# Tap weights computed in quarters of the TensorE array and kept in SBUF, with the products spread one by one

## The chip, the cores and the metric

The kernel runs on one core of one Trainium2 chip. The core's engines are TensorE (PE, with its weight loads shown apart as PEld), VectorE (DVE), ScalarE (ACT), GpSimd (POOL) and SyncE (SP), which here only issues transfers. Each engine works through its own instructions in order and meets the others at semaphores. The metric is the device time of one execution in microseconds, as the median of several runs; less is better. The profile is one execution of its own, and its times are those of that execution.

## The reference, cut to what matters

The input `x` has 8 images of 256 channels and 64 x 64 pixels, fp32. Two layers follow one another, each as `x = x + layer(group_norm(x))`.

Layer 0 makes, for every pixel and every one of 32 channel groups, nine weights ("tap weights") out of a small network, and uses them on the 3 x 3 neighbourhood of a map `x3`:

```
h  = relu(bn2(conv1x1(relu(bn1(concat(x1, unfold3(x2)))), cw1)))   # 32 channels
w  = conv1x1(h, cw2) + cb2                                         # 32 groups x 9 taps
out[group, s] = sum over k of w[group, k] * unfold3(x3)[group, s, k]   # 8 channels s in a group
```

Layer 1 is local attention over 7 x 7 neighbourhoods (queries, keys, values, softmax), plus a branch with nine softmax weights per channel and pixel. In this branch all nine maps are nearly the same, so the kernel needs only one depthwise result times a quotient: with the weights taken relative to tap 4, the sum of eight exponentials plus one, limited to 1e37, and its reciprocal.

## The kernel before, in words

**Bands.** An image is cut into 8 bands (`NB`) of 8 rows, so there are 64 bands. The main loop runs over `g` from -12 to 63. In iteration `g` layer 1 works on band `g`, and layer 0 works ahead of it: the value maps of band `g + 12`, the hidden maps of band `g + 11`, and the tap weights and products of band `g + 10`. For `g` below 0 layer 0 is alone (the "front"). For `g` from 0 to 53 both layers run side by side, and for the last ten bands layer 1 is alone.

**Places.** An iteration has 8 steps `s` (`STEPS`), and each step calls `advance()` six times, so a band has 48 places. There is no automatic scheduling: the order in which the Python code issues instructions is the order in which each engine runs them. `after(n, f)` puts a piece of work `n` places later. `beside(g, s)` returns lists of what runs at the head, middle and end of a step, and `steer(g, s)` issues loads.

**Hidden map.** `hidden_maps` (from L413) ends in `relu` (L440), one ACT instruction that writes the hidden map of a band into `h2n[i % 2]`. This tile has 128 partitions, because the 8 rows of a band are split into 4 quarters of 2 rows, each with its 32 channels on 32 partitions. A row of the tile has two columns of padding, which makes 132 elements.

**Tap weights and products.** `tap_weights` (L463) takes a group of taps: two at a time beside layer 1, three at a time in the front (`TG`, L36). For each tap it issues one matmul (L470) of the block-diagonal 128 x 128 weights `c2[:, tap]` with the hidden map into a PSUM tile `pw`, which comes from the pool `gen` with four buffers, shared with nearly all other matmul results. PE runs a matmul in fp32 as two passes, and the profile counts both. Then `product` (L474) multiplies on DVE (L483): `prod = (pw[tap] + bias) * x3q[shifted]`, for 8 channels and 130 positions. Of its two tensor inputs `pw` lies in PSUM and `x3q` in SBUF. POOL adds the product to `xg` (L491), the sum over the taps. `prod` has two buffers. In the front every third product goes another way: PE adds it up in PSUM (L504). `TAPS_AT` (L67) says at the end of which steps the groups are issued, and `PRODUCTS_AT` (L68) how many places after that each product is. Beside layer 1 these are the ends of steps 1 to 5, and the products come one and two places after. When the last tap is in, `take` (L513) makes statistics and stores the band.

**Branch of layer 1.** `branch_weights` (L882) computes exponentials on ACT (L891) into `ex` (three buffers), POOL adds them up (L1106), and `dynamic_sum` (L893) makes the total (L899), its limit (L902), the reciprocal in two halves on DVE (L907), the two quotients on POOL (L908), and the product with the depthwise result `oc` (L912, L913). `depthwise_end` (L876) writes `oc` on ACT (L879). At the start of a band POOL also copies edges of the small map `x2` (L357 to L364), for which it waits for ACT (L347).

Of the kernel before, what the change touches and what calls it, by code (L numbers as in the profile page):

```python
# [10 lines left out]
F32 = mybir.dt.float32  # L11
# [7 lines left out]
P = 128  # L19
C = 256  # L20
# [16 lines left out]
SHARE = C // REL  # L37
PIECE = SR * W
RUN = (SR - 1) * (W + 2) + W
TG = 2, 3  # L40
HP = W + 2
HR = R + 2

# [20 lines left out]
STEPS = NCT * NT // 2  # L64


TAPS_AT = (1, 2, 3, 4, 5), (0, 2, 4)  # L67
PRODUCTS_AT = ((1, 2),) * 5, ((7, 14, 10), (9, 17, 13), (12, 20, 16))  # L68


CB3, CBQ, CBK, CBP, CWP0, CWP1, CW1, CW2, CBV = 0, 1, 2, 3, 4, 5, 6, 15, 24
# [16 lines left out]
def conv_layers_kernel(ctx: ExitStack, tc: tile.TileContext, ins: dict, out: bass.AP):  # L88
# [19 lines left out]
    def load(name, shape, src=None, now=True):  # L108
        t = const.tile(shape, F32, name=f"c_{name}")
        late.append(lambda: nc.scalar.dma_start(out=t, in_=ins[name] if src is None else src))  # L110
        if now:
            late.pop()()
        return t
# [8 lines left out]
    c1 = load("c1", [P, 3, REL])  # L122
    gq = load("gq", [P, P])
    gc = load("gc", [P, NCT, P])
    c2 = load("c2", [P, KK, P], now=False)
    wq = load("wq", [P, NCT, C], ins["wq"].rearrange("(t p) n -> p t n", p=P), now=False)
    wk = load("wk", [P, NCT, C], ins["wk"].rearrange("(t p) n -> p t n", p=P), now=False)
    wv = load("wv", [P, NCT, C], ins["wv"].rearrange("(t p) n -> p t n", p=P), now=False)
# [10 lines left out]
    x3n = [const.tile([P, R, HP], F32, name=f"x3n_{ct}") for ct in range(NCT)]  # L139

    h2n = [const.tile([P, SR, HP], F32, name=f"h2n_{i}") for i in range(2)]
    for t in probs + x3n + h2n:
        nc.gpsimd.memset(t, 0.0)

    def inverse_root(v):
# [45 lines left out]
    def layer1_loads():  # L191


        last = w1.tile([P, NCT, 1, C], F32, tag="oc", name="last")
        for f in late:
            f()
        nc.scalar.dma_start(out=last, in_=wfc_in[:, :, KK - 1 :])

        def first():
            nc.vector.tensor_scalar(wv, wv, rate1, None, ALU.mult)  # L200

        def difference(kt):
            nc.vector.tensor_sub(wfc[:, kt], wfc[:, kt], last[:, kt].to_broadcast([P, KK - 1, C]))

        return [first, lambda: difference(0), lambda: difference(1)]
# [12 lines left out]
    def after(n, f):  # L220
        later.append((place[0] + n, f))
# [191 lines left out]
    def hidden_maps(b, i, alone):  # L413

        im = images[b]
        hids = []
        h2 = h2n[i % 2][:, :, :W]

        def hidden(t):
            n = P if t == 0 else 96
            hid = w0.tile([P, R, W], F32, tag="hid", name=f"hid_{b}_{i}_{t}", bufs=2)
            nc.scalar.activation(
                hid[:n], im.x2[i][:n, t : t + R, :], AF.Relu, bias=bn1b[:n, t : t + 1], scale=bn1s[:n, t : t + 1]
            )
            hids.append(hid)

        def conv(home, first, last, start, stop):
            ph = home[:, 2 * P : 3 * P].rearrange("p (r c) -> p r c", r=SR)  # L430
            for t in range(first, last):
                n = P if t == 0 else 96
                for q in range(NQR):
                    nc.tensor.matmul(  # L434
                        ph[q * REL : (q + 1) * REL], c1[:n, t], hids[t][:n, q * SR : (q + 1) * SR],
                        start=(t == start), stop=(t == stop),
                    )
            return ph

        def relu(v):  # L440
            nc.scalar.activation(h2, v, AF.Relu, bias=bn2b, scale=bn2s)

        def one(home):
            ph = conv(home, 0, 2, 0, 1)
            after(1, lambda: hidden(2))
            after(2, lambda: nc.scalar.copy(h2, ph))

        def two(home):
            ph = conv(home, 2, 3, 2, 2)
            after(1, lambda: nc.vector.tensor_add(h2, ph, h2))  # L450
# [12 lines left out]
    def tap_weights(b, i, u, alone, at):  # L463


        im = images[b]
        first, n = TG[alone] * u, min(TG[alone], KK - TG[alone] * u)
        pw = ps.tile([P, n, SR * HP], F32, tag="gen", name=f"pw_{b}_{i}_{u}", bufs=4)
        for j in range(n):
            nc.tensor.matmul(  # L470
                pw[:, j], c2[:, first + j], h2n[i % 2].rearrange("p r c -> p (r c)"), start=True, stop=True
            )

        def product(j):  # L474
            k = first + j
            if alone and j == n - 1:
                prod = w1.tile([P, NCT, RP, W], F32, tag="yp", name=f"prod_{b}_{i}_{k}", bufs=3)
                prod = prod.rearrange("p t r c -> p (t r c)")[:, : SHARE * SR * HP]
                prod = prod.rearrange("p (s n) -> p s n", s=SHARE)
            else:  # L480
                prod = w0.tile([P, SHARE, SR * HP], F32, tag="prod", name=f"prod_{b}_{i}_{k}", bufs=2)
            at = k // 3 * HP + k % 3
            nc.vector.scalar_tensor_tensor(  # L483
                prod[:, :, :RUN], pw[:, j, :RUN].unsqueeze(1).to_broadcast([P, SHARE, RUN]),
                par[:, PCB2 + k : PCB2 + k + 1],
                im.x3q[i].rearrange("p s r c -> p s (r c)")[:, :, at : at + RUN], ALU.add, ALU.mult,
            )
            if alone and j == n - 1:
                after(9, lambda: gather(prod))
            else:  # L490
                nc.gpsimd.tensor_add(im.xg[i], im.xg[i], rows(prod))  # L491
            if k == KK - 2 + (not alone):
                if alone:
                    after(13, combine)
                after(14 if alone else 7, take)
# [379 lines left out]

    def depthwise_end(b, i, ct, acc):  # L876

        oc = w1.tile([P, BAND], F32, tag="oc", name=f"oc_{b}_{i}_{ct}")
        nc.scalar.activation(oc, acc.rearrange("p r c -> p (r c)"), AF.Copy, scale=rate2)  # L879
        return oc  # L880

# [11 lines left out]
    def dynamic_sum(b, i, ct, ex, oc):  # L893
# [5 lines left out]
        engine.tensor_add(tot, ex[:, 1], ex[:, 0])  # L899


        engine.tensor_scalar(tot, tot, 1.0, 1.0e37, ALU.add, ALU.min)  # L902
        rec = w1.tile([P, BAND // 2], F32, tag="rec", name=f"rec_{b}_{i}_{ct}", bufs=1)

        def quotient(u):
# [13 lines left out]
                out=out[b].rearrange("(t p) n -> p t n", p=P)[:, :, i * BAND : (i + 1) * BAND], in_=xr  # L919
            )  # L920

        after(9, lambda: quotient(0))
        after(13, lambda: quotient(1))
        after(15, weigh)


    def beside(g, s):
# [57 lines left out]
        if 0 <= g + AHEAD - 1 < B * NB and s == (2 if alone else 1):  # L985
# [5 lines left out]
                    convs.extend(parts)  # L991

            end.append(hidden)
        if 0 <= g + AHEAD - 2 < B * NB and s in TAPS_AT[g < -1]:
            u = TAPS_AT[g < -1].index(s)
            end.append(
                lambda: tap_weights(*divmod(g + AHEAD - 2, NB), u, g < -1, PRODUCTS_AT[g < -1][u])
            )
        return head, mid, end

    def steer(g, s):
# [128 lines left out]
def _layout(inputs):  # L1130
# [29 lines left out]
    arr["par"] = par  # L1160

    c2 = a["a_cw2"].reshape(REL, KK, REL).transpose(2, 1, 0)
    arr["c2"] = np.zeros((P, KK, P), f)
    for q in range(NQR):
        arr["c2"][q * REL : (q + 1) * REL, :, q * REL : (q + 1) * REL] = c2

    chan = np.zeros((C, NCHAN), f)
    chan[:, CB3] = a["a_b3"]
# [43 lines left out]
```

## Time and profile before

| | |
|---|---|
| median of 3 runs | 3852.04 us (3850.59 to 3853.89) |
| the profiled execution's own time | 3854.63 us |
| its span | 3852.8 us |
| instructions | 71646 |
| `pw` matmul passes (L470) | 1152 |
| products (L483), mean of one | 576, 1294 ns |
| additions of products on POOL (L491), mean of one | 549, 2185 ns |

The profile page gives each engine's busy time, the chain of work that ended last, and groups of instructions. In a group's line one reads: line, engine, operation, names of output and inputs, shapes, count, then the busy time in us and the mean of one in ns, and at the end the idle time of the engine just before these instructions and what ended it. Busy time overlaps between engines, so idle time matters only on the engine that sets the end. The timeline view lists instructions in order of time with their start and duration. The view by stretches gives, for a stretch of the execution, the busy time of PE, PEld, DVE, ACT and POOL with the number of instructions, then the granted clock, the share of time that the transfer engines were busy, and GB/s.

### The profile page before, as it was taken

The numbers are of one execution on the slowest core, as the hardware profiler recorded it, in microseconds if no ns is written. First come the engines' busy times: TensorE is split into PE (matmuls) and PEld (weight loads), VectorE is DVE, ScalarE is ACT, GpSimd is POOL, SyncE is SP. The second block draws the span as 40 slices with busy tenths as digits, with TensorE's granted clock in tenths as the row PEclk, the third lists the DMA queues.
The fourth block names the chain that finished last, engine by engine and source line by source line (L and its number), as shares of the span: only waits on it lengthen the run. The fifth ranks groups of instructions, "written<-read, shape, count | busy, mean of one in ns | idle before, by whom it ended". The sixth has DMA issues, their size and how long they took to land.

```text
span 3852.8 us, 71646 instructions
## 1 busy us (share of the span) xinstructions
PE 3756.3 (97%) x24620; PEld 2109.9 (55%) x24620; DVE 3434.4 (89%) x7125; ACT 2809.2 (73%) x6770; POOL 3116.8 (81%) x2100
## 2 busy tenths in 40 slices
PE   6889999999999999999999999999999999999998
PEld 3445555555555555555555555555555555555554
DVE  6879999999999999899998999999999899978877
ACT  4457777777777777777777777777777777677776
POOL 4868888888897888888888888888888888855565
PEclk9999999999999999999999999999999999999999
DMA  8764544544444544544544544454544544232221
GB/s 247 210 177 128 142 118 129 151 126 118 133 135 131 145 123 115 148 135 127 136 116 142 142 125 120 126 149 125 136 115 117 138 119 114 74 97 78 79 67 37
DMA packets 438926, 490.14 MB, mean 127 GB/s; under 512 B 62016, under 2 KB 324256, under 8 KB 438304
## 3 DMA queue, kind: packets, MB, share of 16 engines
q1 hardware_dynamic: 421984, 469.79, 44.1%
q10 hardware_dynamic: 16576, 15.76, 1.3%
q8 instruction: 194, 3.18, 0.4%
q14 instruction: 172, 1.41, 0.1%
HBM read 343.76 MB, written 145.10 MB: 127 GB/s over the span
## 4 chain that ended last, share of the span: by engine, by line
PE 81%; POOL 10%; DVE 3%; DMA 2%; ACT 2%; issue 2%; SPq 1%; ACTq 0%; POOLq 0%; DVEq 0%
PE pf L886 39%; PE small L799 6%; PE ptp L787 6%; POOL xg L491 6%; PE pk L706 5%; PE pq L684 5%; PE sco L750 5%; PE p L375 5%; PE pv L601 5%; PE pw L470 2%; POOL ex L1106 2%; PE small L332 1%; DVE prod L483 1%; PE small L434 1%; DMA x<-x3n 1%
## 5 line engine op out<-in xcount | busy, mean ns | idle before, releaser
L886 PE MATMUL pf<-yp,c_wfc 128*128 128x512 f32 x4096 | 1916.8, 594 | 11.3 <-DVE prod L483 6.3
L491 POOL TENSOR_TENSOR xg<-xg,prod 128x1024 f32<-128x1024 f32 x549 | 1199.8, 2185 | 132.5 <-DVE prod L483 103.6
L886 PEld LDWEIGHTS pf<-yp,c_wfc 128*128 128x128 f32 x4096 | 739.6, 190 | 711.4 <-issue 654.7
L1106 POOL TENSOR_TENSOR ex<-ex,ex 128x1024 f32<-128x1024 f32 x384 | 908.8, 2367 | 68.5 <-ACT ex L891 65.0
L891 ACT ACTIVATE ex<-pf 128x512 f32<-128x512 f32 x1024 | 604.0, 590 | 347.9 <-PE pf L886 269.2
L843 DVE SCALAR_TENSOR_TENSOR acc<-yp,c_chan,acc 128x504 f32<-128x504 f32 (+3 forms) x1104 | 775.5, 702 | 63.2 <-ACT acc L834 42.8
L483 DVE SCALAR_TENSOR_TENSOR prod<-pw,c_par,x3q 128x1040 f32<-128x1040 f32 x576 | 732.7, 1294 | 107.9 <-PE pw L470 60.8
L869 DVE SCALAR_TENSOR_TENSOR acc<-hid,c_chan,acc 128x504 f32<-128x504 f32 (+3 forms) x1024 | 751.1, 733 | 18.1
L781 ACT ACTIVATE prob<-prob,tot 128x196 f32<-128x196 f32 x1024 | 412.9, 452 | 242.4 <-DVE tot L779 236.8
L772 ACT ACTIVATE prob<-prob,nmax 128x196 f32<-128x196 f32 x1024 | 458.2, 450 | 101.3 <-DVE nmax L764 101.2
L907 DVE RECIPROCAL rec<-tot 128x256 f32<-128x256 f32 x256 | 445.7, 1741 | 28.3 <-POOL tot L902 27.5
L789 ACT COPY pt<-ptp 112x512 f32<-112x512 f32 x511 | 295.9, 579 | 111.8 <-PE ptp L787 111.8
L764 DVE CUSTOM_DVE_ANT_0 prob<-sco,c_mask 128x196 f32<-128x196 f32 x1024 | 324.8, 355 | 31.0 <-PE sco L750 31.0
L787 PEld LDWEIGHTS ptp<-ident,prob 128*112 128x112 f32 x2044 | 227.3, 133 | 184.4 <-issue 132.7
L787 PE MATMUL ptp<-ident,prob 128*112 128x128 f32 x2044 | 319.5, 279 | 0.0
L908 POOL TENSOR_TENSOR tot<-tot,rec 128x256 f32<-128x256 f32 x254 | 185.8, 732 | 145.7 <-DVE rec L907 139.7
L799 PEld LDWEIGHTS small<-pt,vt 112*64 112x64 f32 x8144 | 258.6, 138 | 79.8 <-issue 60.5
L799 PE MATMUL small<-pt,vt 112*64 112x64 f32 x8144 | 294.2, 225 | 3.3 <-DMA vt<-vd 1.8
L601 PE MATMUL pv<-c_wv,yp 128*128 128x256 f32 x1056 | 253.5, 383 | 1.8 <-ACT yp L572 1.8
L902 POOL TENSOR_SCALAR tot<-tot 128x512 f32<-128x512 f32 x127 | 243.9, 1920 | 11.1
L470 PEld LDWEIGHTS pw<-h2n,c_c 128*128 128x128 f32 x1152 | 175.1, 191 | 139.9 <-issue 115.9
L375 PE MATMUL p<-xc,w3s 128*128 128x512 f32 x512 | 243.3, 598 | 0.0
(136 smaller groups left out, 4656.7 us busy)
## 6 DMA issues: line engine op xcount, KB each, us to landing
vt<-vd SPq DMA_DIRECT2D x512, 112.0 KB
x3q<-x SPq DMA_DIRECT2D x128, 264.0 KB
xc<-in_x SPq DMA_DIRECT2D x64, 512.0 KB
xg<-in_xg SPq DMA_DIRECT2D x64, 512.0 KB
yp<-x SPq DMA_DIRECT2D x128, 256.0 KB
xr<-x SPq DMA_DIRECT2D x64, 512.0 KB
out_x<-xr SPq DMA_DIRECT2D x64, 512.0 KB
xs<-in_x SPq DMA_DIRECT2D x57, 512.0 KB
```

The lines of the kernel that those rows point to most:

```text
L483: nc.vector.scalar_tensor_tensor(prod[:, :, :RUN], pw[:, j, :RUN].unsqueeze(1).to_broadcast([P, SHARE, RUN]), par[:, PCB2 + k : PCB2 + k + 1],
L491: nc.gpsimd.tensor_add(im.xg[i], im.xg[i], rows(prod))
L601: nc.tensor.matmul(pv[:, g], yp[:, kt, r : r + 2].rearrange("p r c -> p (r c)"), wv[:, kt], start=(kt == 0), stop=(kt == NCT - 1),)
L772: nc.scalar.activation(prob[:, h, :NKEY], prob[:, h, :NKEY], AF.Exp, bias=nmax[:, h : h + 1], scale=-1.0, accum_out=tot[:, h : h + 1],)
L787: nc.tensor.transpose(ptp[:, h, ch], prob[:, h, ch * CHUNK : (ch + 1) * CHUNK], ident)
L799: nc.tensor.matmul(po[half[h], :, t * TQ : (t + 1) * TQ], im.vt[i + ch, m][:n, t, (2 * ct + h) * HD : (2 * ct + h + 1) * HD], pt[:n, h, ch ...
L843: nc.vector.scalar_tensor_tensor(o, yp[:, ct, ra + dr : rb + dr, ca + dc : cb + dc], chan[:, ct, CW1 + k : CW1 + k + 1], o, ALU.mult, ALU.add,
L869: nc.vector.scalar_tensor_tensor(o, hid[:, ra + dr : rb + dr, ca + dc : cb + dc], chan[:, ct, CW2 + k : CW2 + k + 1], o, ALU.mult, ALU.add,)
L886: nc.tensor.matmul(pf, wfc[:, kt, 2 * m + j, ct * P : (ct + 1) * P], images[b].yp[i][:, kt, PAD : PAD + R], start=(kt == 0), stop=(kt == N ...
L891: nc.scalar.activation(ex[:, j].rearrange("p (r c) -> p r c", r=R), pf, AF.Exp)
L907: nc.vector.reciprocal(rec, v)
L1106: after(4, lambda ex=ex, exb=exb: nc.gpsimd.tensor_add(ex, ex, exb))
```

## The change

The weights of a tap are block-diagonal in four blocks of 32. The change cuts the 128 x 128 matmul into four of 64 x 64, each with two of the blocks.

1. `c2` keeps only 64 columns: for each tap, rows 0 to 63 hold the blocks of quarters 0 and 1, rows 64 to 127 those of quarters 2 and 3. The blocks are the same for all quarters.
2. A second hidden map `h2s` holds the two halves of `h2` exchanged. `relu` writes it with two more ACT instructions on 64 partitions each, ahead of the one that writes `h2`.
3. Beside layer 1 there are now two groups of taps instead of five: taps 0 to 3 at the end of the last step of the iteration before, and taps 4 to 8 at the end of step 3 (`TAPS`, `TAPS_AT`). A group has two lots. The first lot uses rows 0 to 63 of the array and the second rows 64 to 127, each with its own PSUM tile; for each output half (64 columns of the array) the map comes from `h2` or `h2s`. So four matmuls of 64 x 64 for two taps stand next to each other. In the front a group still has three taps, all in the first lot.
4. Beside layer 1 `keep` copies the PSUM tiles to an SBUF tile `kept` on ACT, one copy a lot, one place after the matmuls. The products read `kept`, so both of their tensor inputs lie in SBUF. In the front they still read PSUM.
5. The products come one by one, 3, 8, 14 and 20 places after the first group and 2, 5, 8, 11 and 14 after the second.
6. In the last band of an image, for the first half of the channels, the limit on the sum of exponentials (L902) comes 5 places later; the first quotient follows 2 places later than before, the second quotient and the product with `oc` one place later.
7. `oc` (and the start-up tile `last` with the same tag) has one buffer instead of two.

```diff
-TG = 2, 3
+HALF = P // 2
...
-TAPS_AT = (1, 2, 3, 4, 5), (0, 2, 4)
-PRODUCTS_AT = ((1, 2),) * 5, ((7, 14, 10), (9, 17, 13), (12, 20, 16))
+TAPS = (((0, 1), (2, 3)), ((4, 5, 6), (7, 8))), tuple(((k, k + 1, k + 2), ()) for k in (0, 3, 6))
+TAPS_AT = (-1, 3), (0, 2, 4)
+PRODUCTS_AT = ((3, 8, 14, 20), (2, 5, 8, 11, 14)), ((7, 14, 10), (9, 17, 13), (12, 20, 16))
...
-    c2 = load("c2", [P, KK, P], now=False)
+    c2 = load("c2", [P, KK, HALF], now=False)
...
+    h2s = const.tile([P, SR, HP], F32, name="h2s")
-    for t in probs + x3n + h2n:
+    for t in probs + x3n + h2n + [h2s]:
...
         def relu(v):
+            for a, z in ((0, HALF), (HALF, 0)):
+                o, z = slice(a, a + HALF), slice(z, z + HALF)
+                nc.scalar.activation(h2s[o, :, :W], v[z], AF.Relu, bias=bn2b[z], scale=bn2s[z])
             nc.scalar.activation(h2, v, AF.Relu, bias=bn2b, scale=bn2s)
...
-        first, n = TG[alone] * u, min(TG[alone], KK - TG[alone] * u)
-        pw = ps.tile([P, n, SR * HP], F32, tag="gen", name=f"pw_{b}_{i}_{u}", bufs=4)
-        for j in range(n):
-            nc.tensor.matmul(
-                pw[:, j], c2[:, first + j], h2n[i % 2].rearrange("p r c -> p (r c)"), start=True, stop=True
-            )
+        lots = TAPS[alone][u]
+        ks = [k for lot in lots for k in lot]
+        n = len(ks)
+        pws = [
+            ps.tile([P, len(lot), SR * HP], F32, tag="gen", name=f"pw_{b}_{i}_{u}_{r}", bufs=4)
+            for r, lot in enumerate(lots) if lot
+        ]
+        side = [slice(0, HALF), slice(HALF, P)]
+        for m in range(len(lots[0])):
+            for q in range(2):
+                for r, lot in enumerate(lots):
+                    if m < len(lot):
+                        h2 = (h2n[i % 2] if q == r else h2s)[side[r]].rearrange("p r c -> p (r c)")
+                        nc.tensor.matmul(pws[r][side[q], m], c2[side[r], lot[m]], h2, start=True, stop=True)
+        weights = [pw[:, m] for pw, lot in zip(pws, lots) for m in range(len(lot))]
+
+        def keep():
+            kept = w0.tile([P, KK - 4, SR * HP], F32, tag="pw", name=f"kept_{b}_{i}_{u}", bufs=1)
+            for pw, lot, at in zip(pws, lots, (0, len(lots[0]))):
+                nc.scalar.copy(kept[:, at : at + len(lot)], pw)
+            weights[:] = [kept[:, j] for j in range(n)]
+
+        if not alone:
+            after(1, keep)
...
-                prod[:, :, :RUN], pw[:, j, :RUN].unsqueeze(1).to_broadcast([P, SHARE, RUN]),
+                prod[:, :, :RUN], weights[j][:, :RUN].unsqueeze(1).to_broadcast([P, SHARE, RUN]),
...
-        oc = w1.tile([P, BAND], F32, tag="oc", name=f"oc_{b}_{i}_{ct}")
+        oc = w1.tile([P, BAND], F32, tag="oc", name=f"oc_{b}_{i}_{ct}", bufs=1)
...
-        engine.tensor_scalar(tot, tot, 1.0, 1.0e37, ALU.add, ALU.min)
+        def limit():
+            engine.tensor_scalar(tot, tot, 1.0, 1.0e37, ALU.add, ALU.min)
+
+        late = 2 if (i, ct) == (NB - 1, 0) else 0
+        if late:
+            after(5, limit)
+        else:
+            limit()
...
-        after(9, lambda: quotient(0))
-        after(13, lambda: quotient(1))
-        after(15, weigh)
+        after(9 + late, lambda: quotient(0))
+        after(13 + late // 2, lambda: quotient(1))
+        after(15 + late // 2, weigh)
...
-        if 0 <= g + AHEAD - 2 < B * NB and s in TAPS_AT[g < -1]:
-            u = TAPS_AT[g < -1].index(s)
-            end.append(
-                lambda: tap_weights(*divmod(g + AHEAD - 2, NB), u, g < -1, PRODUCTS_AT[g < -1][u])
-            )
+        for gt, st in ((g, s), (g + 1, s - STEPS)):
+            front = gt < -1
+            if 0 <= gt + AHEAD - 2 < B * NB and st in TAPS_AT[front]:
+                u = TAPS_AT[front].index(st)
+                end.append(
+                    lambda gt=gt, u=u, front=front: tap_weights(
+                        *divmod(gt + AHEAD - 2, NB), u, front, PRODUCTS_AT[front][u]
+                    )
+                )
```

More of the change, by code (lines that the diff above doesn't have):

```diff
@@ L191, in layer1_loads @@
     def layer1_loads():
-        last = w1.tile([P, NCT, 1, C], F32, tag="oc", name="last")
+        last = w1.tile([P, NCT, 1, C], F32, tag="oc", name="last", bufs=1)
         for f in late:
@@ L466, in tap_weights @@
         im = images[b]
-        first, n = TG[alone] * u, min(TG[alone], KK - TG[alone] * u)
-        pw = ps.tile([P, n, SR * HP], F32, tag="gen", name=f"pw_{b}_{i}_{u}", bufs=4)
-        for j in range(n):
-            nc.tensor.matmul(
-                pw[:, j], c2[:, first + j], h2n[i % 2].rearrange("p r c -> p (r c)"), start=True, stop=True
-            )
+        lots = TAPS[alone][u]
[20 more added lines that the diff above has]
+            after(1, keep)
         def product(j):
-            k = first + j
+            k = ks[j]
             if alone and j == n - 1:
@@ L1162, in _layout @@
     c2 = a["a_cw2"].reshape(REL, KK, REL).transpose(2, 1, 0)
-    arr["c2"] = np.zeros((P, KK, P), f)
+    arr["c2"] = np.zeros((P, KK, HALF), f)
     for q in range(NQR):
-        arr["c2"][q * REL : (q + 1) * REL, :, q * REL : (q + 1) * REL] = c2
+        o = q * REL % HALF
+        arr["c2"][q * REL : (q + 1) * REL, :, o : o + REL] = c2
     chan = np.zeros((C, NCHAN), f)
```

## The prediction

> **What bounds the kernel now.** I began with the page's share of busy time and the chain that ended last.
>
> ```profile
> PE 3756.3 (97%) x24620; PEld 2109.9 (55%) x24620; DVE 3434.4 (89%) x7125; ACT 2809.2 (73%) x6770; POOL 3116.8 (81%) x2100
> PE 81%; POOL 10%; DVE 3%; DMA 2%; ACT 2%; issue 2%; SPq 1%; ACTq 0%; POOLq 0%; DVEq 0%
> ```
>
> TensorE (PE) sets the end, but DVE and POOL are not far behind. A mean over stages says little, so next came busy time in stretches: the front (47 to 233 us), and the middle of the run, where each band of layer 1 runs beside a band of layer 0 ten bands ahead.
>
> ```profile
> 47.00:233.00 186.00, 152.55 (x748) 79.77 (x748) 156.16 (x169) 86.13 (x160) 146.69 (x106) 0.93 0.75 207
> 1040.00:3220.00 2180.00, 2168.54 (x14443) 1227.93 (x14443) 1998.61 (x4173) 1655.22 (x4001) 1866.04 (x1246) 1.00 0.47 130
> ```
>
> The columns are PE, weight load, DVE, ACT, POOL. In 2180 us of the middle PE lacks 11 us of being always busy, DVE has 181 us to spare, ACT 525, POOL 314. I reckon in this stretch. Layer 1 with products beside it runs from 233 to 3349 us (54 bands of 57.7 us), so a gain or loss here counts 3116 / 2180 = 1.43 times.
>
> Third, the groups of the lines that the change touches, and POOL's waits in the stretch.
>
> ```profile
> L470 PE MATMUL pw<-h2n,c_c 128*128 128x132 f32 x1152 | 182.8, 280 | 1.8 <-ACT ex L891 1.8
> L750 PE MATMUL sco<-kb,qb 64*64 64x196 f32 x4096 | 235.4, 344 | 0.8 <-ACT qb L688 0.8
> L483 DVE SCALAR_TENSOR_TENSOR prod<-pw,c_par,x3q 128x1040 f32<-128x1040 f32 x576 | 732.7, 1294 | 107.9 <-PE pw L470 60.8 <-POOL xg L491 29.8 <-issue 16.1
> L491 POOL TENSOR_TENSOR xg<-xg,prod 128x1024 f32<-128x1024 f32 x549 | 1199.8, 2185 | 132.5 <-DVE prod L483 103.6 <-DVE sc_a L263 2.9 <-DMA yp<-x 2.8
> POOL x L357 <- ACT x L347: 170.1, 38, 6.4
> POOL xg L491 <- DVE prod L483: 57.0, 86, 1.7
> ```
>
> 1152 matmul records are 576 taps in two passes each, and a product per tap. POOL's 314 us of idleness are mostly one hole per band, before L357.
>
> Fourth, the operation that the trace of before nearly lacks: a DVE instruction with both tensor inputs in SBUF. A product today reads `pw` from PSUM. Only L205, in the front, reads two SBUF tensors. DVE's and POOL's instructions in order of time (start us, us):
>
> ```profile
> 55.60 4.20 DVE L205 TENSOR_TENSOR c_wfc<-c_wfc,last 128x2048 f32<-128x2048 f32 x1
> 71.55 2.28 DVE L205 TENSOR_TENSOR c_wfc<-c_wfc,last 128x2048 f32<-128x2048 f32 x1
> ```
>
> ```profile
> 50.97 6.68 POOL L491 TENSOR_TENSOR xg<-xg,prod 128x1024 f32<-128x1024 f32 x3
> 61.16 6.69 POOL L491 TENSOR_TENSOR xg<-xg,prod 128x1024 f32<-128x1024 f32 x3 [3.50 <-DVE prod L483]
> 68.66 2.17 POOL L491 TENSOR_TENSOR xg<-xg,prod 128x1024 f32<-128x1024 f32 x1
> 75.19 6.70 POOL L491 TENSOR_TENSOR xg<-xg,prod 128x1024 f32<-128x1024 f32 x3 [4.36 <-DVE prod L483]
> ```
>
> The same instruction takes 2.28 us while POOL stands idle (70.8 to 75.2), and 4.20 us when it starts 2.05 us before the end of a POOL addition (57.65). It ends 2.15 us after that addition: as if it had stood still until POOL was done. Products with one SBUF input show no such thing: 1.29 us, although most of them run under a POOL addition.
>
> [...] 64x64 scores start four at a time about 6.5 ns apart and a round of four takes 173 ns, while the slot of a 512-column pass grows from 429 to 522 ns when scores follow. [...]
>
> **The change part by part.**
> *Taps on PE.* Today a pass holds PE 113 ns (start to start), so a band costs 18 x 113 = 2034 ns. After, a band has rounds of up to four 64x64 matmuls: four for the first group, six for the second. A score round takes 173 ns for 196 columns, 10 more than the 163 that its columns take at the 429 ns of a 512-column pass; 132 columns take 111, so a round is about 120 and a band 10 x 120 = 1200 ns. Both groups stand directly ahead of scores, so the drain into this mode (93 ns) and the slow first round (224 instead of 173) are paid once, as now. Saved 0.83 us a band, 54 bands: 45 us while PE is the bound.
> *The front.* 27 groups keep three taps each, now 6 rounds of 120 instead of 6 passes of 113 ns, and switch mode alone (93 in, about 50 for the first round, 98 out): +0.28 us, 7.7 us in all. PE is 82% busy there, so 0 to 8; I take 4.
> *ACT.* Two 64-partition relus of about 0.48 us (today's L441 takes 482 ns) and four copies: from L446 (128 elements, 250 ns) and L789 (512, 579) three of 264 elements take 0.37 and one of 396 takes 0.48, so 2.5 us a band. ACT has 525 / 37.7 = 14 us a band to spare. The copies stand ahead of the exponentials of steps 0 and 4 and delay them by 0.7 to 0.85; without that cover the 2.5 us would be added.
> *Products in two SBUF inputs.* In the stretch 339 products start; by the records 87% of them start under a POOL instruction, with 0.79 us of it to run on average, and 1.14 of their 1.29 us overlap POOL. With a lock that overlap goes. DVE: L205 lost 1.92 of 2.05 us, so 0.79 - 0.13 = 0.66 us a product[...]: 1998.6 + 339 x 0.605 = 2204 us. POOL: a product reads for about 1.09 us (2.147 us for 2048 elements after POOL's end, times 1040 / 2048), and 87% hold POOL up: 1866.0 + 339 x 0.87 x 1.09 = 2187 us. Either exceeds the 2180 us that the stretch takes, before any idleness.
> *Places.* Products go one by one, from 3 places into step 0 (48 places a band, 1.2 us each), so the first two additions move into POOL's hole before L357. That absorbs the hole (170 + 32 us with L358), but not the other waits, 71 us for products and exponentials. In an in-order pair that now waits for each other I put remaining POOL idleness at half as much again, 105 us: 2187 + 105 = 2292, or +112 in the stretch, times 1.43 = +160 us. PE's 45 us are then worth nothing: it waits.
> *Late limit, one buffer for `oc` and for `kept`.* In eight bands L902 moves five places, the quotients two and one, the product with `oc` one. ACT's write of the next `oc` (L879) comes 0.7 us or more after POOL's read ends today; one place later or a slower POOL makes ACT wait, with the exponentials behind it. Between -8 and +8 us; I take 0 and leave POOL's lateness in the term above. `kept` is overwritten five places (6 us) after the first group's last product: a DVE more than that late would hold ACT too.
> *DMA queues.* No DMA moves but the store of the finished band, one place later; `x3q` is issued some 20 us ahead of the earlier first product. Half the bytes of `c2` are saved in the front. Nothing for these.
>
> Sum: 3852.8 + 160 + 4 = 4017 on the profiled execution, whose own time is 3854.6, 2.6 above the median of the runs; so I put the median at 4015 us.
>
> **The rivals.** *The lock doesn't hold for this instruction form* (0.20): L205 is one pair of records. Then PE stays the bound and gains 45 less 4: 3811 us, 3795 to 3838. This is the case on the other side; it decides if products keep 1.2 to 1.3 us under POOL's additions. *Contention that the new places mostly dodge* (0.10, of which 0.04 within 0.2%): the run is periodic, so products could regularly start as POOL ends or in its hole. Without extra idleness DVE's 2204 remains, +24 x 1.43: 3845 to 3890. [...] (0.08): POOL's instructions follow one another without a gap, mean 1.50 us (1866.0 / 1246). If half of the products are passed over once, DVE gets 170 x 1.5 = 255 more: 2459, +399 us, about 4250 and above. *ACT becomes the bound* through copies or `oc`: against it 14 us to spare a band; below 0.01 alone.
>
> **How the numbers follow.** Contention as reckoned has 0.62, its own range 3890 to 4250 us. A measurement of this kernel tells about 0.2% (8 us) from no change. Faster 0.20, same 0.04, slower 0.76 (0.62 + 0.08 + 0.06). For 8 in 10 the range takes in dodged contention (0.10), half of the passed-over case and a fifth of the fast one: 3825 to 4330.
>
> **What would show it.** Product records of 1.9 us mean instead of 1.29, with few at 1.24; POOL additions stretched by up to 1.1 us beyond 2.185 or starting late; PE below 97% busy in the middle, waiting on ACT and, behind it, on POOL and DVE; bands of 60 to 62 us; tap rounds of 120 ns. Were products to stay at 1.24 us beside unstretched additions, the prediction would be wrong, and bands near 56.9 us would follow.

## The result, and the profile after

The changed kernel takes 4177.29 us (median of 5 runs, 4169.86 to 4181.11). The kernel before took 3852.04 us in the same comparison. The ratio is 1.084, with an interval of 1.0825 to 1.0856: 325 us slower. The profiled execution's own time is 4179.14 us, its span 4177.3 us.

First the page of the changed kernel: busy time, then the chain that ended last, by engine and by line.

```profile
PE 3829.1 (92%) x25772; PEld 2058.8 (49%) x25772; DVE 3723.9 (89%) x7125; ACT 2920.1 (70%) x7118; POOL 3324.0 (80%) x2101
DVE 34%; PE 24%; POOL 16%; ACT 14%; issue 6%; DMA 5%; SPq 1%; ACTq 0%; POOLq 0%; DVEq 0%
DVE prod L506 13%; PE pf L909 12%; POOL xg L514 7%; DVE acc L892 6%; DVE rec L937 4%; DVE acc L866 4%; POOL ex L1140 3%; POOL tot L922 3%; PE small L822 2%; POOL tot L926 2%; PE sco L773 2%; DVE prob L787 2%; ACT x L349 2%; DMA vt<-vd 2%; ACT prob L804 2%
```

PE carried 81% of the chain before and carries 24% now. No engine has taken its place: DVE, PE, POOL and ACT share the chain, and the product (L506, L483 before) is its largest line. The same stretch of the middle as before, with the columns PE, weight load, DVE, ACT, POOL, then clock, DMA share and GB/s:

```profile
1040.00:3220.00 2180.00, 2011.56 (x13735) 1085.66 (x13734) 1997.58 (x3793) 1559.93 (x3828) 1824.37 (x1132) 0.98 0.44 118
```

PE now lacks 168 us of being always busy where it lacked 11. DVE is as busy as before (1998 us), but gets through 3793 instructions instead of 4173. POOL is less busy than before. In bands, counted from the first score of a band to that of the next, the mean of bands 1 to 52 grows from 57.67 to 63.56 us; in each of them DVE is busy 5.2 us longer (53.0 to 58.2) and POOL 3.7 us (49.7 to 53.4). Bands 0 to 53 take 3429.8 us instead of 3115.8, which is +314 of the +325 us. The front ends 6 us later, and the last ten bands take 4.5 us more.

The groups of instructions that answer to those shown of before, from the page and from the list with shapes kept apart:

```profile
L514 POOL TENSOR_TENSOR xg<-xg,prod 128x1024 f32<-128x1024 f32 x549 | 1217.5, 2218 | 457.4 <-DVE prod L506 428.3
L506 DVE SCALAR_TENSOR_TENSOR prod<-kept,c_par,x3q 128x1040 f32<-128x1040 f32 x495 | 947.8, 1915 | 94.0 <-POOL xg L514 57.9
```

```profile
L485 PE MATMUL pw<-h2n,c_c 64*64 64x132 f32 x1152 | 125.2, 308 | 5.7 <-ACT ex L914 3.2 <-DVE kb L744 2.5
L485 PE MATMUL pw<-h2s,c_c 64*64 64x132 f32 x1152 | 121.6, 308 | 0.6 <-DVE kb L744 0.3
L491 ACT COPY kept<-pw 128x264 f32<-128x264 f32 x165 | 56.9, 381 | 1.5 <-PE pw L485 1.5
```

A product that reads `kept` takes 1915 ns instead of 1294. POOL's own additions are hardly longer (2218 against 2185 ns), but POOL waits 428 us for products where it waited 104. POOL's longer instructions are elsewhere. These three groups, before and then after, are the total of the exponentials, its limit and the last sum of the branch:

```profile
L902 POOL TENSOR_SCALAR tot<-tot 128x512 f32<-128x512 f32 x127 | 243.9, 1920 | 11.1
L913 POOL TENSOR_TENSOR xr<-xr,oc 128x512 f32<-128x512 f32 x127 | 161.9, 1275 | 10.0
L899 POOL TENSOR_TENSOR tot<-ex 128x512 f32<-128x512 f32 x127 | 161.7, 1273 | 9.9
```

```profile
L926 POOL TENSOR_SCALAR tot<-tot 128x512 f32<-128x512 f32 x127 | 321.4, 2531 | 11.1
L922 POOL TENSOR_TENSOR tot<-ex 128x512 f32<-128x512 f32 x127 | 210.9, 1661 | 10.0
L943 POOL TENSOR_TENSOR xr<-xr,oc 128x512 f32<-128x512 f32 x127 | 196.6, 1548 | 10.0
```

None of the three was edited in its work, only the place of the limit in eight bands. They now take 0.27 to 0.61 us longer.

Why that is so can be seen in single instructions. The timeline of the changed kernel (start and duration in us), DVE first, then POOL:

```profile
724.40 3.09 DVE L506 SCALAR_TENSOR_TENSOR prod<-kept,c_par,x3q 128x1040 f32<-128x1040 f32 x1
727.41 0.35 DVE L787 CUSTOM_DVE_ANT_0 prob<-sco,c_mask 128x196 f32<-128x196 f32 x1
```

```profile
724.03 2.35 POOL L1140 TENSOR_TENSOR ex<-ex,ex 128x1024 f32<-128x1024 f32 x1
726.47 2.15 POOL L922 TENSOR_TENSOR tot<-ex 128x512 f32<-128x512 f32 x1
```

The product starts 0.37 us after a POOL instruction that ends at 726.38. It ends at 727.49, 1.11 us after that, as if it had begun to read only then. POOL's next instruction, L922, starts at 726.47, takes 2.15 us where it took 1.27 before, and ends 1.13 us after the product. Each has stood still for the other. Which of the two goes first, the starts in the records don't tell at close range, as a second place in the same trace shows:

```profile
670.58 3.32 DVE L506 SCALAR_TENSOR_TENSOR prod<-kept,c_par,x3q 128x1040 f32<-128x1040 f32 x1 [1.75 <-POOL xg L514]
```

```profile
668.36 4.44 POOL L514 TENSOR_TENSOR xg<-xg,prod 128x1024 f32<-128x1024 f32 x2
```

The second of POOL's two additions runs from 670.62 to 672.80 in the single records. It starts 44 ns after the product, and yet the product ends 1.10 us after it, so POOL went first.

The waits over the whole run show whom the longer products hold up. Before:

```profile
POOL xg L491 <- DVE prod L483: 103.6, 132, 4.5
ACT prob L781 <- DVE tot L779: 236.8, 202, 2.6
ACT prob L772 <- DVE nmax L764: 101.2, 111, 4.8
```

After (total us, times, longest):

```profile
POOL xg L514 <- DVE prod L506: 428.3, 258, 4.3
ACT prob L804 <- DVE tot L802: 515.7, 313, 3.9
ACT prob L795 <- DVE nmax L787: 345.7, 149, 5.6
POOL x L359 <- ACT x L349: 73.6, 55, 27.9
```

The softmax alternates between engines: DVE finds the maxima, ACT makes exponentials, DVE the reciprocals, ACT scales, PE multiplies. A product that stands in DVE's queue ahead of a maximum or a reciprocal delays ACT, and behind ACT PE. These two ACT waits grew by 523 us together. POOL's hole before L359 (L357 before), 284 us long, shrank to 74 us, since the first additions moved into it.

### The profile page after: what moved, and what is told of

The parts are those of the page before. It is cut to its first block, busy times and chain, and to the rows that moved or that the text cites. A ratio compares the mean times of both kernels' runs of the same rounds, so it can differ in the third digit from the quotient of the medians.

```text
span 4177.3 us, 74178 instructions
## 1 busy us (share of the span) xinstructions
PE 3829.1 (92%) x25772; PEld 2058.8 (49%) x25772; DVE 3723.9 (89%) x7125; ACT 2920.1 (70%) x7118; POOL 3324.0 (80%) x2101
## 4 chain that ended last, share of the span: by engine, by line
DVE 34%; PE 24%; POOL 16%; ACT 14%; issue 6%; DMA 5%; SPq 1%; ACTq 0%; POOLq 0%; DVEq 0%
DVE prod L506 13%; PE pf L909 12%; POOL xg L514 7%; DVE acc L892 6%; DVE rec L937 4%; DVE acc L866 4%; POOL ex L1140 3%; POOL tot L922 3%; PE small L822 2%; POOL tot L926 2%; PE sco L773 2%; DVE prob L787 2%; ACT x L349 2%; DMA vt<-vd 2%; ACT prob L804 2%
## 5 line engine op out<-in xcount | busy, mean ns | idle before, releaser
L909 PE MATMUL pf<-yp,c_wfc 128*128 128x512 f32 x4096 | 1971.8, 610 | 97.7 <-ACT ex L914 85.0
L514 POOL TENSOR_TENSOR xg<-xg,prod 128x1024 f32<-128x1024 f32 x549 | 1217.5, 2218 | 457.4 <-DVE prod L506 428.3
L909 PEld LDWEIGHTS pf<-yp,c_wfc 128*128 128x128 f32 x4096 | 757.0, 194 | 860.1 <-issue 649.8
L506 DVE SCALAR_TENSOR_TENSOR prod<-kept,c_par,x3q 128x1040 f32<-128x1040 f32 x495 | 947.8, 1915 | 94.0 <-POOL xg L514 57.9
L1140 POOL TENSOR_TENSOR ex<-ex,ex 128x1024 f32<-128x1024 f32 x384 | 907.3, 2363 | 58.2 <-ACT ex L914 53.8
L926 POOL TENSOR_SCALAR tot<-tot 128x512 f32<-128x512 f32 x127 | 321.4, 2531 | 11.1
L938 POOL TENSOR_TENSOR tot<-tot,rec 128x256 f32<-128x256 f32 x254 | 197.8, 779 | 159.8 <-DVE rec L937 153.7
L729 PE MATMUL pk<-yp,c_wk 128*128 128x512 f32 (+2 forms) x576 | 242.5, 548 | 8.0 <-DVE bias L320 8.0
```

The lines of the kernel that those rows point to most:

```text
L506: nc.vector.scalar_tensor_tensor(prod[:, :, :RUN], weights[j][:, :RUN].unsqueeze(1).to_broadcast([P, SHARE, RUN]), par[:, PCB2 + k : PCB2 ...
L909: nc.tensor.matmul(pf, wfc[:, kt, 2 * m + j, ct * P : (ct + 1) * P], images[b].yp[i][:, kt, PAD : PAD + R], start=(kt == 0), stop=(kt == N ...
L1140: after(4, lambda ex=ex, exb=exb: nc.gpsimd.tensor_add(ex, ex, exb))
```

## The experiments

Theory A is the prediction's: a product with two SBUF inputs and a POOL instruction hold each other up, as in the 1.11 and 1.13 us above (in what follows, the lock), and this alone makes the kernel slower. Rivals: the copies and the new places cost it (B), or the late limit (C). Under A a second question is what the lock costs through: DVE's longer time, POOL's longer time, or the way the two alternate.

In kernels made from the one before, `oc` has one buffer, as in the change, where the added tile needs the room.

### Copies unread, and copies read

To the kernel before:

```diff
+        kept = w0.tile([P, n, SR * HP], F32, tag="kept", name=f"kept_{b}_{i}_{u}", bufs=1)
+        if not alone:
+            nc.scalar.copy(kept, pw)
```

and, in the second kernel only,

```diff
-                prod[:, :, :RUN], pw[:, j, :RUN].unsqueeze(1).to_broadcast([P, SHARE, RUN]),
+                prod[:, :, :RUN], (pw if alone else kept)[:, j, :RUN].unsqueeze(1).to_broadcast([P, SHARE, RUN]),
```

> The kernel before, with ACT copying every group of tap weights beside layer 1 to SBUF (two taps a copy, issued right behind the matmuls) and nobody reading the copy; the products still read PSUM. One buffer for oc. Theory of the lock (two SBUF inputs of a product make DVE and POOL wait for each other): 3850 to 3870 us, products at 1.29 us, since ACT has 14 us a band to spare. Rival (the copies or the single oc buffer hold ACT up, and TensorE behind it): above 3900 us.

> The same, but the products beside layer 1 read the copy, so both of their tensor inputs lie in SBUF; matmuls of 128 x 128, five groups and the places of the products as before. Theory of the lock: products of 1.8 to 2.0 us on average and 4050 to 4200 us. Rival (the loss of the change comes from quarters, from the new places or from the late limit): 3850 to 3880 us, like the kernel whose copy nobody reads, and products at 1.24 to 1.30 us.

Measured: 4099.30 us unread (ratio 1.0632, 1.0616 to 1.0648) and 4506.38 us read (1.1688, 1.1672 to 1.1704). The first was not the free control that it was meant to be: its time falls to its rival's side. The group of the products in the kernel with unread copies:

```profile
L487 DVE SCALAR_TENSOR_TENSOR prod<-pw,c_par,x3q 128x1040 f32<-128x1040 f32 x576 | 733.7, 1297 | 419.8 <-ACT kept L476 380.3 <-PE pw L470 10.1 <-DMA x3q<-x 7.6
```

The product keeps its 1297 ns, but waits 380 us for an ACT copy that it doesn't read. The two read the same PSUM tile, and in this build the second reader came out ordered behind the first. With the copies read:

```profile
L487 DVE SCALAR_TENSOR_TENSOR prod<-kept,c_par,x3q 128x1040 f32<-128x1040 f32 x495 | 1057.0, 2153 | 394.6 <-ACT kept L476 374.4 <-POOL xg L495 6.7 <-issue 6.3
```

The wait for the copy is the same (374 us), so the pair still tells one thing: the source of one operand alone takes the product from 1297 to 2153 ns and the time by 407 us. 495 products by 0.856 us are 424 us. Both the products and the time lie above the 1.8 to 2.0 us and the 4050 to 4200 us expected of the lock.

### Quarters of the array, products from PSUM

The changed kernel's quarters and `h2s`, without copies and without the late limit, in four groups directly ahead of scores, each product one to three places after its group; the front as before, and one buffer for `oc` as in the change.

```diff
-TAPS_AT = (1, 2, 3, 4, 5), (0, 2, 4)
-PRODUCTS_AT = ((1, 2),) * 5, ((7, 14, 10), (9, 17, 13), (12, 20, 16))
+TAPS = (((0,), (1,)), ((2,), (3,)), ((4,), (5,)), ((6, 7), (8,))), tuple(((k, k + 1, k + 2), ()) for k in (0, 3, 6))
+TAPS_AT = (-1, 1, 3, 5), (0, 2, 4)
+PRODUCTS_AT = ((1, 2), (1, 2), (1, 2), (1, 2, 3)), ((7, 14, 10), (9, 17, 13), (12, 20, 16))
...
+                        nc.tensor.matmul(
+                            pws[r][side[q], m], c2[side[r], lot[m], side[r]], h2, start=True, stop=True
+                        )
```

> Quarters of the array without the copy: four groups of two, two, two and three taps, each directly ahead of scores (ends of steps 7, 1, 3 and 5), the second hidden map as in the change, the products read PSUM one, two and three places later; 128 x 128 matmuls in the front as before; one buffer for oc. Theory of the lock: TensorE gets back 10 rounds of 120 ns for 18 passes of 113, 0.83 us a band, so 3800 to 3820 us. Rival (quarters themselves cost, by changes of mode, by two PSUM buffers held at once or by the extra relus): 3860 us or more.

Measured: 3850.62 against 3855.33 us, ratio 0.9987 (0.998 to 0.9993). The loss is gone, but only 5 us of PE's gain appear, so the time lies between the two cases expected. The stretch of the middle and the chain by engine in this kernel:

```profile
1040.00:3220.00 2180.00, 2145.24 (x15134) 1181.43 (x15133) 1992.47 (x4184) 1689.24 (x4084) 1873.86 (x1250) 1.00 0.48 130
```

```profile
PE 57%; DVE 19%; ACT 8%; POOL 6%; issue 4%; DMA 3%; SPq 2%; ACTq 0%; POOLq 0%; DVEq 0%
```

PE's work got shorter, and PE idles 35 us in the stretch where it idled 11. DVE has 19% of the chain instead of 3%. The other engines take over as soon as PE has a little less to do.

### What PE's time is worth

The kernel before with one of two tap matmuls beside layer 1 left out; both products then read the first.

```diff
-        for j in range(n):
+        for j in range(n if alone else 1):
...
-                prod[:, :, :RUN], pw[:, j, :RUN].unsqueeze(1).to_broadcast([P, SHARE, RUN]),
+                prod[:, :, :RUN], pw[:, j if alone else 0, :RUN].unsqueeze(1).to_broadcast([P, SHARE, RUN]),
```

> The kernel before with only the first tap's matmul of each group of two beside layer 1; both products read its result. TensorE issues 4 matmuls (8 passes of 113 ns, 0.90 us a band) less, about what quarters save, and nothing else moves. Left out: four of nine taps' matmuls. If TensorE's time is worth its full length, as the prediction had it: 3855 - 54 x 0.90 = 3806 us, 3800 to 3815. If another engine takes over as the bound at once: 3835 to 3855 us.

Measured: 3840.83 us, ratio 0.9972 (0.9962 to 0.9981). Four taps of two passes by 113 ns are 0.90 us a band and 49 us in 54 bands; the time fell by 12. So a microsecond of PE is worth about a quarter of a microsecond here, although PE was 99% busy in the middle. In the stretch of the middle PE idles 24 us where it idled 11:

```profile
1040.00:3220.00 2180.00, 2155.63 (x14229) 1200.90 (x14228) 2007.36 (x4188) 1659.70 (x4016) 1875.66 (x1252) 1.00 0.48 130
```

### The lock taken out of the changed kernel

In the changed kernel the products beside layer 1 are replaced by two statistics instructions of about the same time together, each with one SBUF input: one reads `kept`, the other `x3q`. The product tiles are cleared once and stay, and POOL adds them as before. Everything else of the change stays.

```diff
-            nc.vector.scalar_tensor_tensor(
-                prod[:, :, :RUN], weights[j][:, :RUN].unsqueeze(1).to_broadcast([P, SHARE, RUN]),
...
+            else:
+                flat = im.x3q[i].rearrange("p s r c -> p (s r c)")
+                k0 = min(j, 1)
+                for e, src in enumerate((whole[0][:, 132 * k0 : 132 * k0 + (512 if n > 4 else 396)],) + (flat[:, :512],) * 1):
+                    nc.vector.bn_stats(prod[:, e, :6], src)
```

> The changed kernel with every product beside layer 1 replaced by two statistics instructions on DVE, of 396 or 512 elements of the copied weights and of 512 elements of x3q, one SBUF input each, about 1.15 us together in place of a product's 1.21 us, with the same waits; POOL's additions, copies, places and everything else as in the change. Left out: the tap products themselves. If the two SBUF inputs are all that costs: 3800 to 3880 us. If the rest of the change (copies on ACT ahead of exponentials, places, groups of PSUM buffers) carries the 179 us that lost time on DVE and POOL in the kernel before didn't explain: 3980 us or more.

Measured: 3858.04 us, ratio 1.001 (1.0003 to 1.0017). Busy time in this kernel, and the two largest of the three groups that stand for the products:

```profile
PE 3723.6 (97%) x25772; PEld 2036.7 (53%) x25772; DVE 3385.4 (88%) x7620; ACT 2924.0 (76%) x7118; POOL 3122.3 (81%) x2103
L527 DVE BATCH_NORM_STATS2 prod<-x3q 128x6 f32<-128x512 f32 x495 | 335.2, 677 | 0.0
L527 DVE BATCH_NORM_STATS2 prod<-kept 128x6 f32<-128x512 f32 x275 | 189.7, 690 | 88.4 <-POOL xg L531 67.0 <-ACT kept L495 21.3
```

The same copies, places, late limit and buffers, without an instruction in two SBUF inputs, take as long as the kernel before to within 0.2%. Removing the products in two SBUF inputs is worth 4177 - 3858 = 319 us. Not quite all of this need be the lock. The two statistics overlap, and DVE is busy 49 us less than in the kernel before (3385.4 against 3434.4 us). At the rate that a filler on DVE shows in this arrangement below (194 us of time for 287 us of work), these 49 us could hide some 33 us, an estimate. So the lock costs between 286 and 319 us by this estimate, and B and C together, less what PE gains, at most a tenth of the loss.

### The late limit

In the changed kernel `late = 0`; and the other way round, the late limit in the kernel with quarters and products from PSUM.

```diff
-        late = 2 if (i, ct) == (NB - 1, 0) else 0
+        late = 0
```

> The changed kernel with the limit where it was before in all bands. If the late limit is next to nothing beside the lock: within 8 us of the changed kernel's 4177. If it cost or saved much in its eight bands (2 us each or more): 16 us away or more.

> The kernel with quarters and products from PSUM, with the change's late limit as well: in an image's last band, first half of the channels, the limit five places later, the quotients two and one, the product with oc one. In the trace without it the last bands take 61.7 to 63.4 us (60.8 before), with DVE's reciprocal waiting for POOL's limit and products and scores queued behind it. If that wait is the cause, the last bands fall to 60 us or less and the kernel to 3825 to 3840 us. Rival (the last bands are slow for another reason, such as PSUM buffers held by the taps): within 0.1% of the one without, 3847 to 3855 us.

Measured: 4190.02 us without it (ratio 1.0878, 1.0863 to 1.0894), 13 us more than with it; and 3856.06 us (1.0005, 0.9996 to 1.0013) with it in the other kernel, 5 us more than without. Neither number is the late limit's own effect. In the profiled executions the front, which these edits don't touch, ends 8.2 us later in the changed kernel without the late limit (247.8 us instead of 239.6), and 4.6 us later in the other kernel with it (238.7 instead of 234.1). From the first score on, the late limit saves 4 us in the changed kernel and costs 4 to 5 us in the other. By bands it does what it says in both: an image's last band (mean of the first six) falls from 66.5 to 61.5 us, and from 62.3 to 61.2. Against that stands the run's very last band, with nothing beside it to cover the wait: 60.8 instead of 57.8 us, and 60.3 instead of 57.4. (For the other kernel the last bands were expected at 60 us or less, so the limit explains less of them than was thought.) C is out as a cause.

### DVE's time, POOL's time, and both

Three kernels from the one before: an extra DVE instruction of one SBUF input behind each product, an extra POOL copy behind each addition, and both. Their results are read by nothing.

```diff
+                nc.vector.bn_stats(idle, v[:, :512])
```

```diff
+                nc.gpsimd.tensor_copy(scratch[:, :270], im.x3q[i].rearrange("p s r c -> p (s r c)")[:, :270])
```

> The kernel before, with one more DVE instruction behind every product beside layer 1: statistics of 512 elements of x3q, one SBUF input, 0.60 us each, written to a scratch tile that nobody reads. It costs DVE what the change costs it (products went from 1.29 to 1.91 us), but holds POOL up in nothing. If DVE's lost time is what makes the changed kernel slow: 4100 to 4180 us. If POOL's lost time (as the prediction's sum had it) makes it: 3900 us or less, as DVE's 1999 + 339 x 0.60 = 2202 us then only just pass the 2180 us of the stretch.

> The kernel before with one more POOL instruction behind each addition beside layer 1, a copy of 270 elements to scratch, an estimated 0.41 us: the 3.7 us a band by which POOL's busy time grew in the changed kernel, with DVE left alone; one buffer for oc. If DVE's lost time makes most of the loss: 3900 us or less. If POOL's lost time does, as the prediction's sum had it: 4000 us or more.

> Both fillers together: 0.60 us more on DVE behind each product and 0.41 us more on POOL behind each addition, still no instruction with two SBUF inputs. DVE's filler alone gave 4003 us. If lost time on the two engines is all that the lock does: 4120 to 4200 us, near the changed kernel's 4177. If the lock hurts by when it stops DVE (long single waits ahead of the softmax) rather than by how much: 4090 us or less.

Measured: 4003.04 us (1.0383, 1.0368 to 1.0397), 3935.39 us (1.0212, 1.0198 to 1.0226), and 3997.95 us (1.0378, 1.0362 to 1.0394). The first two lie between the cases expected, so in this order neither engine's lost time alone, evenly spread, makes the loss. Busy time in them:

```profile
PE 3814.4 (95%) x24620; PEld 2118.0 (53%) x24620; DVE 3699.9 (93%) x7620; ACT 2783.0 (70%) x6770; POOL 3121.4 (78%) x2100
PE 3781.4 (96%) x24620; PEld 2115.6 (54%) x24620; DVE 3437.6 (87%) x7125; ACT 2805.6 (71%) x6770; POOL 3283.1 (83%) x2595
```

DVE's busy time grew by 266 us and the run by 148; POOL's by 166 and the run by 81. Both together cost no more than DVE's alone. Half of an added microsecond reaches the end, although DVE and POOL both had idle time to put it in; and the two losses don't add up.

The same was then done on the changed kernel without the lock: a third statistics instruction for each product, then the POOL copy as well.

```diff
-                for e, src in enumerate((...) + (flat[:, :512],) * 1):
+                for e, src in enumerate((...) + (flat[:, :512],) * 2):
```

> The same with a third statistics instruction of 512 elements of x3q a product: 0.60 us more of DVE's time, as much as the lock adds on average to a product, but evenly and without holding POOL up. Left out: the tap products. If the amount of DVE's lost time sets the time in this arrangement: 4120 to 4200 us. If the single long waits (up to 4.7 us) or POOL's stops matter as well: 4080 us or less.

> The changed kernel with statistics in place of products (one SBUF input), the 0.60 us filler on DVE and, behind every addition beside layer 1, a copy of 270 elements on POOL, about 0.41 us. DVE's filler alone gave 4053 us, the changed kernel 4177. Left out: the tap products. If the remaining 124 us are POOL's lost time: 4140 to 4200 us. If they come from the uneven, long single waits that only the lock makes: within 30 us of 4053.

Measured: 4052.55 us (1.051, 1.0492 to 1.0527) and 4076.67 us (1.059, 1.0573 to 1.0606). Waits of the first, to be held against those of the changed kernel:

```profile
ACT prob L821 <- DVE tot L819: 575.0, 375, 4.4
POOL xg L531 <- DVE prod L527: 320.7, 174, 3.9
ACT prob L812 <- DVE nmax L804: 197.9, 142, 2.5
```

287 us of DVE time (3672.3 - 3385.4 busy), spread evenly, cost 194 us and bring up the same wait of ACT for DVE. POOL's time adds 24. That is 219 of the 319 us. By what was expected, the last 100 us would all come from uneven waits, but two other terms can be estimated. DVE is busy 50 us less with both fillers than in the changed kernel (3674.2 against 3723.9), which is the shortfall named above and at the same rate (194 / 287) makes about 34 us. And PE's clock, shown in the last section, gives at most some 41 us. The rest, some 25 us, would be the unevenness: products of up to 4.7 us, and single waits of ACT for a maximum of up to 5.6 us against 2.5 and 2.9 us in the filled kernels. That last share is left over by elimination, and no run isolates it; it stays open.

## Why the prediction was right or wrong

The direction was right, and 4177 us lies inside the range of 3825 to 4330 us. That range was wide, and its centre, 4015 us, holds only half of the loss.

*The lock: right.* From one pair of L205 records the prediction took that two SBUF inputs stand still behind POOL, +0.605 us a product (0.66 reckoned from the records, less 0.055 by which a product alone was to get shorter, see the small terms) and an end about 1.09 us after POOL's. The records of bands 0 to 52 show 1.907 us mean against 1.295, so +0.612, and typically 1.10 us. That the means agree so closely is in part luck: 65% of the products start under a POOL instruction, not 87%, and the products that POOL passed over (below) help to make up for it. That the lock doesn't hold for this form (0.20) is refuted by the source of one operand alone (+407 us) and by taking the products in two SBUF inputs out (-319 us).

*The size: half of it, and the step at fault is the one that turned stall time into run time.* It set each engine's work against the 2180 us of the stretch, took POOL as the bound with 2187 us, added 105 us of idleness, and got +112 in the stretch, +160 in the run. The measured term is 314 us in bands 0 to 53. Two things failed in it.

First, POOL was not blocked 0.95 us (0.87 x 1.09) by a product, but 0.41 us: its busy time grew by 3.7 us a band. An addition usually has waited for the product itself and so doesn't meet the next one; the limit, the total and the last sum do. Of the prediction's two signs for POOL, stretched additions came true for few (17 of the 432 between 240 and 3300 us, by 0.3 us or more), and additions that start late for many (POOL waited 258 times for a product).

Second, and this decides: the sum let idle time absorb the stalls, and asked only for what exceeds it. DVE got 5.2 us of work more a band, the band 5.9 us longer; DVE's idle time went from 4.7 to 5.3 us a band and POOL's from 8.0 to 10.2. The idle time is made of waits in a chain that alternates between DVE, ACT and PE, and under the lock it stayed. The fillers show a part of this in kernels without any lock: about half, and in the changed order two thirds, of DVE's added time reaches the end, and idle time takes up the rest (with the DVE filler in the kernel before, DVE idles 2.5 us a band).

In the prediction's stretch of 2180 us, which is 37.8 bands of before, the two errors read: POOL's work 2018 us instead of 2187, its idleness 386 instead of 105. They have opposite signs, so that the sum came as near as half of the loss is luck too.

*PE's 45 us: the saving on PE was real, its worth was not.* In the kernel with the lock taken out, where PE seldom waits, 16 score passes alone take 852 ns, with the first group of taps ahead of them 1300 and with the second 1519 (medians, taps included). The pass ahead of the scores holds PE 93 to 94 ns longer in all three. So a band's taps cost 448 + 667 = 1115 ns, and some 0.9 us are saved where 0.83 was reckoned. But "while PE is the bound" failed: PE 99% busy was worth a quarter of its time (12 of 49 us). So the rival at 3811 us was out of reach even without a lock: the two kernels nearest to it take 3851 us (products from PSUM) and 3858 us (lock taken out). In the changed kernel itself the gain was taken as worth nothing, so this didn't move the forecast.

*Dodged contention* (0.10) didn't happen: 162 of 477 products stay below 1.35 us, too few. *Passed over* (0.08) happened in part: 47 of 477 products were overtaken by a whole POOL instruction (3.08 us mean), where that rival had half of them. It accounts for part of the mean.

*Small terms.* The front ends 6.0 us later, inside the 0 to 8, but the four other kernels with the same front give 6 to 14, so one record says little. Copies take 0.38 us for the forecast 0.37, ACT has room for them, and with all the rest of the change they cost no more than the 33 us estimated above. An uncontended product takes 1283 ns at least, and not the author's estimate of 1240. A line through two DVE instructions of the kernel before that had two SBUF inputs and an idle POOL beside them (L912 at the very end, 512 elements, 693 ns; the second L205, 2048 elements, 2281 ns) gives 1239 ns for 1040 elements, also an estimate; for the product, with one row of weights broadcast over eight maps, the gain of 55 ns doesn't show. The late limit was put at -8 to +8 and taken as 0; from the first score on it saves 4 in the changed kernel and costs 4 to 5 in the other.

*Signs.* Products of 1.9 us mean, PE waiting on ACT and behind it DVE, PE at 92% in the middle: as written. Bands of 60 to 62 us: 63.6.

## What to carry to other kernels

Before a matmul result is copied to SBUF for VectorE, count the SBUF inputs of the instruction that will read it: where the other input is in SBUF too and GpSimd is busy, leaving the operand in PSUM was worth 286 to 319 us here. Don't let an engine's idle share pay for a stall before you have asked what it waits for; where engines alternate in one chain, measure with a filler instruction what added time is worth. Here even fillers passed on half to two thirds of it, and the uneven stalls of the lock lengthened a band by more than they added to DVE (5.9 against 5.2 us). And test what the bound is worth in the same way, by leaving some of its work out: a PE that was 99% busy returned a quarter of what was taken off it.

## What the runs showed of the hardware

- Which of the two goes first when both start together isn't settled by the start in the records: a POOL addition that began 44 ns after the product still went ahead of it, and one product was passed over by two POOL instructions and took 4.67 us.
- The lock works in both directions. Products went from 1294 to 1915 ns mean, and POOL's limit, an operation in one tensor, from 1920 to 2531 ns.
- PE's granted clock dropped to half in the middle of the run. Between 300 and 3300 us the kernel before has no record of half clock, and the changed kernel has 33 stretches, 150 us in all, at 92% busy. They begin on a grid of 3.41 us. No wait of PE was longer than 3.24 us, but in the interval ahead of each of the 32 that begin after 300 us PE had idled for 1.78 us or more, mostly in two waits. Idle times of up to 1.86 us were not always enough. In the kernel before, PE idles 1.07 us at most in such an interval. The kernel with the lock taken out has none at 97%; with DVE's filler it has 19 stretches (68 us), and with both fillers 17 (79 us), at 93%. Half of the difference to the last, (150 - 79) / 2, is 36 us, an estimate of what the lower clock cost; counted to the end of band 53, (171 - 89) / 2 is the 41 us named above. The two waits of matmuls that grew most in the changed kernel are these.

```profile
PE pf L909 <- ACT ex L914: 85.0, 81, 2.1
PE ptp L810 <- ACT qb L711: 67.8, 36, 2.5
```

- Two engines that read one PSUM tile came out ordered in this build: 380 us of waiting for a copy whose result the waiting instruction didn't use.
